# Products of a constant put into fresh PSUM tiles where a task planner foresees idle TensorE (sparse attention and non-local layer, one core)

## The chip, the cores and the metric

The kernel runs on one core of one Trainium2 chip. The metric is the device time of one execution in microseconds (us). Every run lists its own time; one execution is also recorded by the hardware profiler, and the views below (the page, the chain of waits, the timeline, the windows, the groups of instructions) are of that execution. All times in the views count from its first instruction.

## The reference

Two layers, one after the other, on an input `x` of 2 x 256 x 64 x 64 (batch, channels, height, width), all in float32. N is 64*64 = 4096.

```
# layer 0
y   = conv3x3(x, 64 output channels) ; batch norm ; PReLU          -> e  [64, N]
sim = e^T e                                                        -> [N, N]
p   = sparsemax(sim, each row)       # max(sim - tau, 0), tau from the sorted row
x   = x p + x
# layer 1
g     = x^T g_w + g_b                # [N, 128]
a, bs = (w_t theta(x)), (w_p phi(x)) # one number for each position
f     = relu(a[:, None] + bs[None, :] + wf_b)
x     = batchnorm(wz (f / N) g) + x
```

The kernel never builds most of `sim`. It takes each row of `sparsemax` as the row's own position alone unless the row has another entry near its maximum; it looks for such rows first (the survey), and works out fully only the rows that it has listed (at most 512 in a batch item). For layer 1 it sorts the `bs` of batch item 0 (and of half of item 1) by counting, so that `relu` becomes a difference of running sums; the other half of item 1 is computed as it stands. A last count says whether a dense version of everything is needed; in the runs here it is not.

## The kernel before, in words

**The planner.** The order of work is set while the kernel is built. `plan.task` (L106) records a task: a function, a cost in us on one or more engines (P is TensorE), a rank, the tasks it follows, and, for a task that opens a PSUM or a work tile, a hold on a ring (`Ring`, L79). `plan.run` (L164) is a list scheduler: at every step `begin` (L141) works out when each open task could start, and `pick` (L152) chooses; then the task's function issues its instructions.

```
    def begin(self, t, e):
        at = max(t.ready[e], self.free[e])
        if t.take:
            ...
            at = max(at, f + self.LAG)
        return at
```

So the planned start `at` is the latest of three: the engine is free, what the task follows has ended, and the ring has a free slot. Nothing of the plan's times gets into the program; only the order does. Each engine's instructions stand in that order in its own queue, and semaphores hold an instruction until its operands are there and its tile is free.

**PSUM.** `ps_sim` (L203, tag `sim`) has 3 buffers of two banks, `ps_av` (L204, tag `av`) has 2 buffers of one bank. `ring_sim` and `ring_av` (L282) stand for them in the plan. A tile's first product waits until the last reader of the buffer's earlier tile has ended.

**The stages.** Times in brackets are those of the profiled execution.

- Setup and the convolution of item 0 (`conv`, L340; products on L362 into `cv` tiles; 0 to about 66). ScalarE and VectorE take a finished pair of `cv` tiles to `e` (`scaled` L372 and L373, `outer` L378, `into_e` L383 to L388). In between, `weight_products` (L260) makes six products with one column each into the tile `pw` (L265 to L268), and `weight_biases` (L275) two into `pc`.
- The survey of item 0 (`survey`, L475; from about 44 to 199), between the tasks of item 1's convolution. Each unit is a 128 x 1024 block of `sim`: two products into a `sim` tile (`unit`, L467; products on L472, called `sv`), a running maximum by column on VectorE (L501 for the first, then L503, into `xbs`), and a sum of excess over a threshold on ScalarE (L507, in place). L512 takes rows' maxima on VectorE. `turned` (L518) transposes the maxima into `ct` (L521). `listing` (L569 to L575) makes the flags.
- The list of rows (`listed`, L580): counts in `pp` (L589 to L591), places on VectorE (L596 to L622), then eight rounds of `low_places` on VectorE (L638, `ohl`) and `numbers` on TensorE (L650, tile `pj`, two `ohl` buffers), then the indices (L656 to L660). GpSimd fetches rows of `e` and `x` (L666, L670) and masks `x` in place (`doubled`, L720).
- The listed rows (`rows`, L728): products `rw` (L472), copied to `z` by ScalarE (L745), maxima and threshold on VectorE (L748 to L762), relu (L768, L770). `attend` (L787) multiplies them into `x` (tile `av`, L794, added by L801); `project` (L817) makes `g` (L825, taken out by L831). Item 1's survey runs among these from about 208 to 349, its list around 354, its rows and `attend` from 374 to 495.
- The ranks (`Ranked`, from L932): `as_row` (L869) turns a column into a row (`pt`, L876, L880), DMA spreads it over all partitions (`kb`), and ScalarE (L992) and VectorE (L997, L1004) count for each key the keys above it (454 to 563). GpSimd scatters and fetches rows (L1026, L1112), `pk` (L1095) places, `yr` (L1132) transposes. Meanwhile TensorE does `project_in` (L845, products on L851) and the plain half, `py` (L1407), fed by ScalarE's `f` (L1397).
- The last products, `pz` (`finish`, L900; L912), are scaled and added by VectorE (L916) and stored, to 725.

The constant `onesq`, a 128 x 128 tile of ones, is written on VectorE by `constants` (L1258), before item 0's convolution is done.

Of the kernel before, what the change touches and what calls it, by code (L numbers as in the profile page):

```python
# [40 lines left out]
TH = 16  # L41
NR = 16
HH = HW // 2
PARTS = [(0, 17), (17, 33), (33, 49), (49, 64)]


# [47 lines left out]
class Plan:  # L94
# [6 lines left out]
    def __init__(self):  # L101
        self.free = {e: 0.0 for e in "PDAGS"}
        self.open = {e: [] for e in "PDAGS"}
        self.count, self.now, self.left = 0, 0.0, 0

    def task(self, cost, fn, rank=0, after=(), lat=0.0, take=None, free=None, **engines):  # L106

# [56 lines left out]
    def run(self, until=lambda: False):  # L164
        while self.left and not until():
            c = [(b[0], e, b[1]) for e in self.open for b in [self.pick(e)] if b]
            assert c, [t.fn for e in self.open for t in self.open[e]]
            at, e, t = min(c, key=lambda x: x[:2])
            for o in t.cost:
                self.open[o].remove(t)  # L170
            self.now = max(self.now, at)
            t.start, t.end, t.engine = at, at + t.cost[e], e
            self.free[e] = t.end
            self.left -= 1
            if t.take:
# [15 lines left out]
def sparse_path(ctx: ExitStack, tc, a, out, rows_i):  # L191
# [51 lines left out]
    wb = tp[:, 2].rearrange("p (d o) -> p d o", d=2)  # L243
    wc = tp[:, 3].rearrange("p (k o) -> p k o", k=CT)

    def weights():

        nc.vector.tensor_scalar_add(s1, v1[:, 4, :], EPS)
        nc.scalar.activation(s1, s1, AF.Sqrt)
        nc.vector.reciprocal(s1, s1)  # L250
        nc.vector.tensor_mul(s1, s1, v1[:, 1, :])
        nc.vector.tensor_sub(b1, v1[:, 0, :], v1[:, 3, :])
        nc.vector.tensor_mul(b1, b1, s1)
        nc.vector.tensor_add(b1, b1, v1[:, 2, :])
        for d in range(2):
            nc.vector.tensor_copy(wb[:, d], vci[:, 2 + d : 3 + d].to_broadcast([P, CI]))
        for kc in range(CT):
            nc.vector.tensor_copy(wc[:, kc], b1[:, kc : kc + 1].to_broadcast([P, CI]))

    def weight_products():  # L260


        pw = ps_av.tile([P, 2, CT + 1], F32, name="pw", tag="av")
        for kc in range(CT):
            nc.tensor.matmul(pw[:, 0, kc : kc + 1], lhsT=ph_sb[:, ts(kc, P)], rhs=vci[:, 3:4], start=True, stop=True)  # L265
            nc.tensor.matmul(pw[:, 1, kc : kc + 1], lhsT=th_sb[:, ts(kc, P)], rhs=vci[:, 2:3], start=True, stop=True)
        nc.tensor.matmul(pw[:, 0, CT : CT + 1], lhsT=wb[:, 0], rhs=vci[:, 0:1], start=True, stop=False)
        nc.tensor.matmul(pw[:, 0, CT : CT + 1], lhsT=wb[:, 1], rhs=vci[:, 1:2], start=False, stop=True)  # L268
        nc.vector.tensor_copy(gw_sb[:, :, CI], pw[:, 0, 0:CT])
        nc.vector.tensor_copy(gw_sb[:, :, CI + 1], pw[:, 0, 0:CT])  # L270
        nc.vector.tensor_copy(gw_sb[:, :, CI + 2], pw[:, 1, 0:CT])
        nc.vector.tensor_add(gb_sb[:, CI : CI + 1], pw[:, 0, CT : CT + 1], vci[:, 4:5])
        nc.vector.memset(gb_sb[:, CI + 1 : CG], 0.0)

    def weight_biases():  # L275
        pc = ps_av.tile([P, CG], F32, name="pc", tag="av")
        for kc in range(CT):
            nc.tensor.matmul(pc, lhsT=wc[:, kc], rhs=gw_sb[:, kc], start=(kc == 0), stop=(kc == CT - 1))
        nc.vector.tensor_sub(gb_sb, gb_sb, pc)
# [60 lines left out]
    def conv(b, parts, rank, ready):  # L340
# [12 lines left out]

        def taps_of(jp, g, n, j, dy):
            if (g, n, dy) == (g, 0, 1):
                d[jp, g] = ps_av.tile([P, 2, R * HH], F32, name=f"cv_{b}_{jp}_{g}", tag="av")
# [62 lines left out]
    def thresholds(b, e_of, there, rank):  # L419
# [6 lines left out]

        def turned(jp):
            e = e_of()
            ps = d[jp, "ps"] = ps_sim.tile([P, 2, 4, P], F32, name=f"tr_{b}_{jp}", tag="sim")
# [37 lines left out]
    def unit(b, e, name, lhs, q):  # L467


        ps = ps_sim.tile([P, UN], F32, name=f"{name}_{b}_{q}", tag="sim")  # L470
        for h in range(2):
            nc.tensor.matmul(ps[:, ts(h, CB)], lhsT=lhs(h), rhs=e[ts(h, CR), q], start=True, stop=True)  # L472
        return ps

    def survey(b, e_of, both, there, copied, limited, accs, rank, ready):  # L475
# [40 lines left out]
            (row_top if e == "D" else rows_over)(i, q)  # L516

        def turned(q, g, acc):  # L518
            ps = d["turn", q, g] = ps_av.tile([P, 4, P], F32, name=f"ct_{b}_{q}_{g}", tag="av")
# [60 lines left out]
    def listed(b, et, flag_of, saved, flagged, got, rank, free_mask, free_ec):  # L580
# [4 lines left out]

        def counts():
            flag = flag_of()
            pp = d["pp"] = ps_av.tile([P, 3, P], F32, name=f"pp_{b}", tag="av")
            nc.tensor.matmul(pp[:, 0, 0:NT], lhsT=tri, rhs=flag, start=True, stop=True)  # L589
            nc.tensor.matmul(pp[:, 1, 0:NT], lhsT=onesq, rhs=flag, start=True, stop=True)  # L590
            nc.tensor.transpose(pp[0:NT, 2], flag, ident)  # L591
# [52 lines left out]

        def numbers(g):
            if g == 0:
                d["pj"] = ps_av.tile([P, 3, KB], F32, name=f"pj_{b}", tag="av")
            for t in range(NT // 8):
                m = NT // 8 * g + t
                nc.tensor.matmul(  # L650
# [28 lines left out]
            nc.scalar.copy(d["eb"][:, :, 1], d["eb"][:, :, 0])  # L679

        def turned():
            pe = d["pe"] = ps_av.tile([P, KB, P], F32, name=f"pe_{b}", tag="av")
# [104 lines left out]
    def attend(b, got, done, halves, xb_ready, rank):  # L787
# [2 lines left out]

        def product(j, ct, k):
            if k == 0:
                pss[j, ct] = ps_av.tile([P, CB], F32, name=f"av_{b}_{j}_{ct}", tag="av")
# [23 lines left out]
    def project(b, ga_of, last, rank):  # L817
# [1 line left out]
        projected, d = {}, {}  # L819

        def product(m0, m1):
            ps = d[m0] = ps_av.tile([P, 3, CG], F32, name=f"g_{b}_{m0}", tag="av")
            for m in range(m0, m1):
                for kc in range(CT):
                    nc.tensor.matmul(  # L825
# [18 lines left out]

    def project_in(b, ga, m0, m1):  # L845

        ps = ps_sim.tile([P, 2, CB], F32, name=f"g_{b}_{m0}", tag="sim")
# [21 lines left out]
    def as_row(name, column, t0, nt, rank, after):  # L869
# [2 lines left out]
        d = {}  # L872

        def turned():
            d["pt"] = ps_av.tile([P, P], F32, name=f"pt_{name}_{t0}", tag="av")
            nc.tensor.transpose(d["pt"][0:nt], column()[:, t0 : t0 + nt], ident)  # L876

        def copied():
# [21 lines left out]
    def finish(b, cols, scaled, engine, rank, after, free):  # L900
# [7 lines left out]

        def product(ct):
            if ct == 0:  # L910
                d["z"] = ps_sim.tile([P, CT, CB], F32, name=f"pz_{b}_{cols.start}", tag="sim")
# [20 lines left out]
    class Ranked:  # L932
# [126 lines left out]
                nc.vector.tensor_add(at(t), at(t), at(t - 1))  # L1059

        def before(self):
            self.po = ps_av.tile([P, CB], F32, name=f"po_{self.b}", tag="av")
# [26 lines left out]
        def places(self, i):  # L1089

            b, R = self.b, self.R
            if i % 2 == 0:
                self.pk[i // 2] = ps_av.tile([P, 8, R + 1], F32, name=f"pk_{b}_{i}", tag="av")
# [25 lines left out]
        def taken(self, i, rank, rest=None):  # L1119
# [8 lines left out]

            def turned(t):
                if t % 4 == 0:  # L1130
                    d["ps"] = ps_av.tile([P, 4, P], F32, name=f"yr_{b}_{i}", tag="av")
# [124 lines left out]

    def constants():
        nc.vector.memset(onesq, 1.0)  # L1258
        nc.gpsimd.affine_select(
            out=tri, in_=onesq, pattern=[[1, P]], compare_op=ALU.is_gt, fill=0.0, base=0, channel_multiplier=-1  # L1260
        )
# [140 lines left out]

    def pair_py(q, m):
        if m == NR:
            pys[q] = ps_sim.tile([P, UN], F32, name=f"py_{q}", tag="sim")
        for h in range(2):
            nc.tensor.matmul(  # L1407
                pys[q][:, ts(h, CB)],
# [31 lines left out]
    )  # L1440
    plan.run()

    pf = ps_av.tile([1, B * (1 + KB)], F32, name="pf", tag="av")
# [395 lines left out]
```

## Time and profile before

| | before |
|---|---|
| time, median of 3 runs | 735.35 us (734.71 to 736.77) |
| the profiled execution's own time | 737.18 us |
| its span, first to last instruction | 735.4 us |
| TensorE matmul busy | 636.2 us (87%), 2783 instructions |
| VectorE / ScalarE / GpSimd busy | 559.1 us / 398.2 us / 203.5 us |
| TensorE clock granted, mean | 0.938 of full |

A float32 product appears in the profile as two MATMUL instructions and two weight loads; a transpose appears as one. "Idle before, by" in a view names what ended an engine's idle time. PEclk is the clock that TensorE was granted; in this profile it is either 1.00 or 0.50.

### The profile page before, as it was taken

Reading aid. Unit: us, or ns where it says so; the run is one execution under the profiler, and the core shown is the slowest. Engines: PE = TensorE matmul, PEld = TensorE weight load, DVE = VectorE, ACT = ScalarE, POOL = GpSimd, SP = SyncE. Lnnn points to the kernel's source line nnn. Section 1 sums busy time; section 2 is a strip of 40 time slices with the busy share of each in tenths; the row PEclk is TensorE's granted clock in tenths of the full one; section 3 lists DMA queues with packets and bytes.
Section 4 is the critical chain, followed back from the end, with each engine's and each line's share of the span. In section 5 each row is a group of like instructions: output and inputs, shape, how many; then the busy total and the mean of one; then the engine's idle time right before and its main releaser. Section 6 shows DMA issues by size and latency. Waiting matters only on the chain.

```text
span 735.4 us, 8191 instructions
## 1 busy us (share of the span) xinstructions
PE 636.2 (87%) x2783; PEld 312.3 (42%) x2783; DVE 559.1 (76%) x1025; ACT 398.2 (54%) x552; POOL 203.5 (28%) x252
## 2 busy tenths in 40 slices
PE   5989979999876979999897959996798998979683
PEld 4656444444322323333544524445443644534341
DVE  6875787677788998786746485999999987772463
ACT  0122647766555877666031352999999865414010
POOL 0006930000048000000083000152445323777240
PEclk9999999999979899999998969998899899979898
DMA  9512010001021000000110002011425345654364
GB/s 353 185 43 59 2 29 15 15 15 30 15 65 29 1 1 1 0 1 0 59 37 0 0 1 115 8 37 37 138 99 136 98 159 201 218 162 107 129 226 152
DMA packets 32984, 54.75 MB, mean 74 GB/s; under 512 B 12850, under 2 KB 19876, under 8 KB 32036
## 3 DMA queue, kind: packets, MB, share of 16 engines
q1 hardware_dynamic: 27252, 40.60, 16.5%
q0 software_dynamic: 5248, 12.94, 6.5%
q10 hardware_dynamic: 432, 0.59, 0.3%
q8 instruction: 24, 0.39, 0.2%
q14 instruction: 28, 0.23, 0.1%
HBM read 31.94 MB, written 20.07 MB: 71 GB/s over the span
## 4 chain that ended last, share of the span: by engine, by line
PE 50%; DVE 23%; ACT 12%; issue 6%; POOL 4%; DMA 4%; DVEq 0%; ACTq 0%; POOLq 0%; SPq 0%
PE sv L472 16%; ACT junk L992 9%; PE av L794 7%; PE cv_in L362 6%; PE cv_out L362 6%; PE py L1407 4%; DVE junk L997 4%; POOL r L1112 4%; DVE mq L748 4%; DVE xbs L503 4%; PE pz L912 3%; PE g L825 2%; DVE z L754 2%; DMA r<-tb,k 2%; DVE z L770 2%
## 5 line engine op out<-in xcount | busy, mean ns | idle before, releaser
L507 ACT ACTIVATE sv<-sv,nthr 128x1024 f32<-128x1024 f32 x134 | 145.9, 1090 | 93.7 <-DVE xbs L503 47.8
L472 PE MATMUL sv<-e 64*128 64x512 f32 x640 | 162.7, 627 | 7.3 <-ACT sv L507 7.3
L794 PE MATMUL av<-z,xbs 128*128 128x512 f32 x256 | 124.2, 627 | 15.5 <-DVE z L770 15.0
L503 DVE TENSOR_TENSOR xbs<-sv,xbs 128x1024 f32<-128x1024 f32 x90 | 110.1, 1224 | 29.6 <-PE sv L472 24.2
L1407 PE MATMUL py<-f,ga 128*128 128x512 f32 x256 | 120.7, 624 | 3.4 <-ACT f L1397 3.4
L992 ACT ACTIVATE junk<-kb,bound 128x640 bf16<-128x640 f32 (+30 forms) x58 | 96.5, 1665 | 8.7 <-DMA kb<-rd_k 8.7
L1397 ACT ACTIVATE f<-ab,ga 128x1024 f32<-128x1024 f32 x64 | 71.3, 1142 | 47.3 <-PE py L1407 47.2
L472 PEld LDWEIGHTS sv<-e 64*128 64x128 f32 x640 | 55.7, 189 | 92.6 <-ACT sv L507 49.9
L1026 POOL DMA_INDIRECT sg<-ga,rank x48 | 49.9, 1041 | 148.3 <-DVE junk L1004 104.0
L794 PEld LDWEIGHTS av<-z,xbs 128*128 128x128 f32 x256 | 47.5, 197 | 82.4 <-issue 55.6
L1112 POOL DMA_INDIRECT r<-tb,k x64 | 61.2, 957 | 59.1 <-PE yr L1132 20.7
L997 DVE TENSOR_SCALAR_CACHE_REDUCE junk<-kb,ga 128x128 bf16<-128x128 f32 (+29 forms) x36 | 76.6, 2162 | 0.2
L666 POOL DMA_INDIRECT eb<-et,idx x8 | 7.9, 983 | 243.8 <-DVE idx L660 129.2
L1407 PEld LDWEIGHTS py<-f,ga 128*128 128x128 f32 x256 | 49.5, 200 | 59.8 <-issue 52.7
L362 PE MATMUL cv_out<-v,wu 128*64 128x256 f32 (+1 forms) x384 | 48.8, 397 | 7.4 <-DVE v L324 7.4
L362 PE MATMUL cv_in<-v,wu 128*64 128x256 f32 (+1 forms) x384 | 49.0, 398 | 4.9 <-DVE col L524 3.9
L1125 DVE SCALAR_TENSOR_TENSOR r<-r,a 128x128 f32<-128x128 f32 x64 | 21.6, 350 | 31.3 <-DMA r<-tb,k 31.0
L801 DVE SCALAR_TENSOR_TENSOR x<-av,b,x 128x512 f32<-128x512 f32 x32 | 23.7, 747 | 27.7 <-PE av L794 26.1
L745 ACT COPY z<-rw 128x1024 f32<-128x1024 f32 x32 | 30.5, 1026 | 26.1 <-PE av L794 17.3
L362 PEld LDWEIGHTS cv_out<-v,wu 128*64 128x64 f32 x384 | 30.4, 142 | 29.0 <-issue 12.5
L912 PE MATMUL pz<-yT,wz_sb 128*128 128x512 f32 x64 | 33.3, 662 | 9.4 <-DVE yT L1139 8.1
L512 DVE MAX8 top<-sv 128x8 f32<-128x1024 f32 x26 | 32.0, 1231 | 12.2 <-PE sv L472 11.8
(202 smaller groups left out, 752.4 us busy)
## 6 DMA issues: line engine op xcount, KB each, us to landing
out<-x SPq DMA_DIRECT2D x32, 256.0 KB, 2.1
tb<-tab SPq DMA_DIRECT2D x3, 2056.0 KB
x<-in_x SPq DMA_DIRECT2D x8, 512.0 KB, 8.7
tab<-sg SPq DMA_DIRECT2D x3, 1040.0 KB, 7.6
x<-in_x SPq DMA_DIRECT2D x4, 544.0 KB
e<-e SPq DMA_DIRECT2D x16, 128.0 KB, 3.2
et<-es SPq DMA_DIRECT2D x16, 128.0 KB, 1.9
mask<-kd SPq DMA_DIRECT2D x2, 1024.0 KB, 4.6
```

The costliest lines, as they stand in the source:

```text
L362: nc.tensor.matmul(d[jp, g][ts(h, CR), n, (r0 - r) * HH : (r1 - r) * HH], lhsT=taps(j, kc, dy), rhs=v[:, kc, r0 + dy - 1 : r1 + dy - 1], s ...
L472: nc.tensor.matmul(ps[:, ts(h, CB)], lhsT=lhs(h), rhs=e[ts(h, CR), q], start=True, stop=True)
L503: nc.vector.tensor_tensor(out=acc, in0=d[i, q], in1=acc, op=ALU.max)
L507: nc.scalar.activation(ps, ps, AF.Relu, bias=both["nthr"][:, i : i + 1], accum_out=got_s["over"][:, i, q : q + 1])
L794: nc.tensor.matmul(pss[j, ct], lhsT=got["xb"][:, k, ts(ct, P)], rhs=got["zs"][k][:, ts(j, CB)], start=(k == 0), stop=(k == KB - 1),)
L912: nc.tensor.matmul(d["z"][:, ct], lhsT=wz_sb[:, ts(ct, P)], rhs=d["y"], start=True, stop=True)
L992: nc.scalar.activation(self.junk[:, 0, c0:c1], kb[:, c0:c1], AF.Sign, scale=STEEP, bias=self.bound[:, d, t : t + 1], accum_out=cnt[:, t, d ...
L997: nc.vector.tensor_scalar(self.junk[:, 1, c0:c1], kb[:, c0:c1], self.key[:, t : t + 1], None, (ALU.is_ge, ALU.is_gt)[d], ALU.add, accum_ou ...
L1026: rows = nc.gpsimd.indirect_dma_start(out=self.sg, out_offset=bass.IndirectOffsetOnAxis(ap=self.rank[:, t : t + 1], axis=0), in_=self.ga[: ...
L1112: nc.gpsimd.indirect_dma_start(out=self.r[:, t % TH], out_offset=None, in_=self.tb, in_offset=bass.IndirectOffsetOnAxis(ap=self.k[:, t : t ...
L1397: nc.scalar.activation(f[0][:, m % 4, :], ab1[0][:, ts(q, UN)], AF.Relu, bias=ga1[0][:, m, CI : CI + 1])
L1407: nc.tensor.matmul(pys[q][:, ts(h, CB)], lhsT=ga1[0][:, m, 0:CI], rhs=f[0][:, m % 4, ts(h, CB)], start=(m == NR), stop=(m == NT - 1),)
```

## The change

`Plan.run` keeps in `plan.gap` how long the chosen task's engine is planned to stand idle ahead of it. A new function `fresh` makes every PSUM tile that `ps_av.tile` or `ps_sim.tile` made before. Once `onesq` has been written (`warm` is then not empty), and where `plan.gap` is long enough, it first issues n products of `onesq` with the first columns (at most 128) of `onesq` into the new tile, each with `start=True, stop=True`. The first true product of the tile, which has `start=True` too, comes behind them and overwrites.

```
+EACH, FROM, MOST = 0.27, 0.3, 24
...
+            self.gap = at - self.free[e]
...
+    def fresh(pool, shape, dtype, name, tag):
+
+        ps = pool.tile(shape, dtype, name=name, tag=tag)
+        n = min(MOST, int((plan.gap - FROM) / EACH))
+        if n > 0 and shape[0] == P and warm:
+            v = ps
+            if len(shape) > 2:
+                axes = " ".join("abc"[: len(shape) - 1])
+                v = ps.rearrange(f"p {axes} -> p ({axes})")
+            wide = min(P, v.shape[1])
+            for _ in range(n):
+                nc.tensor.matmul(v[:, 0:wide], lhsT=onesq, rhs=onesq[:, 0:wide], start=True, stop=True)
+        return ps
+
+    warm = []
...
-        pw = ps_av.tile([P, 2, CT + 1], F32, name="pw", tag="av")
+        pw = fresh(ps_av, [P, 2, CT + 1], F32, name="pw", tag="av")
...
     def constants():
         nc.vector.memset(onesq, 1.0)
+        warm.append(True)
```

All other calls of `ps_av.tile` and `ps_sim.tile` in the sparse path are edited like that of `pw`. The planned costs and times are not touched, so the instructions of VectorE, ScalarE, GpSimd and SyncE are the same in the same order, and so are those of TensorE but for 113 added products ahead of 30 tiles. Those are, in TensorE's order (the time is that of the tile's first true product in the profile of before):

```
tile (item)       products  columns   at us      tile (item)      products  columns   at us
pw                      11        6   48.13      av_7_1 (0)              3      128  411.52
ct_3_0 (0)               6      128  182.03      rw, k=1, q=3 (1)        4      128  426.38
pp (0)                  11      128  198.99      g_30 (0)                3      128  439.69
pj (0)                   8       12  204.13      av_1_0 (1)              2      128  446.08
sv, i=1, q=1 (1)         8      128  210.64      pt (a row of item 0)    1      128  495.16
sv, next unit (1)        2      128  212.50      g_0 (1)                 1      128  495.30
rw, q=1 (0)              1      128  226.84      g_6 (1)                 5      128  497.99
rw, q=2 (0)              3      128  228.93      pt (a row of item 1)    4      128  508.02
sv, q=0 (1)              2      128  252.80      g_18 (1)                8      128  512.20
sv, q=2 (1)              5      128  265.70      py_0                    4      128  519.90
ct_3_1 (1)               3      128  350.23      py_1                    4      128  553.66
pp (1)                   1      128  354.08      pz_0 (1)                3      128  681.94
av_3_1 (0)               2      128  358.39      pz_2560 (1)             1      128  701.56
g_12 (0)                 1      128  365.67      pz_3584 (1)             1      128  707.36
g_21 (0)                 3      128  401.97      pz_3584 (0)             2      128  721.96
```

More of the change, by code (lines that the diff above doesn't have):

```diff
@@ L103, in __init__ @@
         self.open = {e: [] for e in "PDAGS"}
-        self.count, self.now, self.left = 0, 0.0, 0
+        self.count, self.now, self.left, self.gap = 0, 0.0, 0, 0.0
     def task(self, cost, fn, rank=0, after=(), lat=0.0, take=None, free=None, **engines):
@@ L275, in weight_biases @@
     def weight_biases():
-        pc = ps_av.tile([P, CG], F32, name="pc", tag="av")
+        pc = fresh(ps_av, [P, CG], F32, name="pc", tag="av")
         for kc in range(CT):
@@ L355, in taps_of @@
             if (g, n, dy) == (g, 0, 1):
-                d[jp, g] = ps_av.tile([P, 2, R * HH], F32, name=f"cv_{b}_{jp}_{g}", tag="av")
+                d[jp, g] = fresh(ps_av, [P, 2, R * HH], F32, name=f"cv_{b}_{jp}_{g}", tag="av")
             v = pair_of(b, j)
@@ L428, in turned @@
             e = e_of()
-            ps = d[jp, "ps"] = ps_sim.tile([P, 2, 4, P], F32, name=f"tr_{b}_{jp}", tag="sim")
+            ps = d[jp, "ps"] = fresh(ps_sim, [P, 2, 4, P], F32, name=f"tr_{b}_{jp}", tag="sim")
             for i in range(4):
@@ L467, in unit @@
     def unit(b, e, name, lhs, q):
-        ps = ps_sim.tile([P, UN], F32, name=f"{name}_{b}_{q}", tag="sim")
+        ps = fresh(ps_sim, [P, UN], F32, name=f"{name}_{b}_{q}", tag="sim")
         for h in range(2):
@@ L518, in turned @@
         def turned(q, g, acc):
-            ps = d["turn", q, g] = ps_av.tile([P, 4, P], F32, name=f"ct_{b}_{q}_{g}", tag="av")
+            ps = d["turn", q, g] = fresh(ps_av, [P, 4, P], F32, name=f"ct_{b}_{q}_{g}", tag="av")
             for k in range(4):
@@ L587, in counts @@
             flag = flag_of()
-            pp = d["pp"] = ps_av.tile([P, 3, P], F32, name=f"pp_{b}", tag="av")
+            pp = d["pp"] = fresh(ps_av, [P, 3, P], F32, name=f"pp_{b}", tag="av")
             nc.tensor.matmul(pp[:, 0, 0:NT], lhsT=tri, rhs=flag, start=True, stop=True)
@@ L646, in numbers @@
             if g == 0:
-                d["pj"] = ps_av.tile([P, 3, KB], F32, name=f"pj_{b}", tag="av")
+                d["pj"] = fresh(ps_av, [P, 3, KB], F32, name=f"pj_{b}", tag="av")
             for t in range(NT // 8):
@@ L681, in turned @@
         def turned():
-            pe = d["pe"] = ps_av.tile([P, KB, P], F32, name=f"pe_{b}", tag="av")
+            pe = d["pe"] = fresh(ps_av, [P, KB, P], F32, name=f"pe_{b}", tag="av")
             for k in range(KB):
@@ L792, in product @@
             if k == 0:
-                pss[j, ct] = ps_av.tile([P, CB], F32, name=f"av_{b}_{j}_{ct}", tag="av")
+                pss[j, ct] = fresh(ps_av, [P, CB], F32, name=f"av_{b}_{j}_{ct}", tag="av")
             nc.tensor.matmul(
@@ L821, in product @@
         def product(m0, m1):
-            ps = d[m0] = ps_av.tile([P, 3, CG], F32, name=f"g_{b}_{m0}", tag="av")
+            ps = d[m0] = fresh(ps_av, [P, 3, CG], F32, name=f"g_{b}_{m0}", tag="av")
             for m in range(m0, m1):
@@ L845, in project_in @@
     def project_in(b, ga, m0, m1):
-        ps = ps_sim.tile([P, 2, CB], F32, name=f"g_{b}_{m0}", tag="sim")
+        ps = fresh(ps_sim, [P, 2, CB], F32, name=f"g_{b}_{m0}", tag="sim")
         pv = ps[:, :, 0 : 3 * CG].rearrange("p d (m c) -> p d m c", c=CG)
@@ L874, in turned @@
         def turned():
-            d["pt"] = ps_av.tile([P, P], F32, name=f"pt_{name}_{t0}", tag="av")
+            d["pt"] = fresh(ps_av, [P, P], F32, name=f"pt_{name}_{t0}", tag="av")
             nc.tensor.transpose(d["pt"][0:nt], column()[:, t0 : t0 + nt], ident)
@@ L910, in product @@
             if ct == 0:
-                d["z"] = ps_sim.tile([P, CT, CB], F32, name=f"pz_{b}_{cols.start}", tag="sim")
+                d["z"] = fresh(ps_sim, [P, CT, CB], F32, name=f"pz_{b}_{cols.start}", tag="sim")
             nc.tensor.matmul(d["z"][:, ct], lhsT=wz_sb[:, ts(ct, P)], rhs=d["y"], start=True, stop=True)
@@ L1061, in before @@
         def before(self):
-            self.po = ps_av.tile([P, CB], F32, name=f"po_{self.b}", tag="av")
+            self.po = fresh(ps_av, [P, CB], F32, name=f"po_{self.b}", tag="av")
             nc.tensor.matmul(self.po[:, 0:CS], lhsT=tri, rhs=self.tab[-1][:, TH - 1], start=True, stop=True)
@@ L1092, in places @@
             if i % 2 == 0:
-                self.pk[i // 2] = ps_av.tile([P, 8, R + 1], F32, name=f"pk_{b}_{i}", tag="av")
+                self.pk[i // 2] = fresh(ps_av, [P, 8, R + 1], F32, name=f"pk_{b}_{i}", tag="av")
             for t in range(4):
@@ L1130, in turned @@
                 if t % 4 == 0:
-                    d["ps"] = ps_av.tile([P, 4, P], F32, name=f"yr_{b}_{i}", tag="av")
+                    d["ps"] = fresh(ps_av, [P, 4, P], F32, name=f"yr_{b}_{i}", tag="av")
                 nc.tensor.transpose(d["ps"][:, t % 4], self.r[:, t % TH, 0:CI], ident)
@@ L1404, in pair_py @@
         if m == NR:
-            pys[q] = ps_sim.tile([P, UN], F32, name=f"py_{q}", tag="sim")
+            pys[q] = fresh(ps_sim, [P, UN], F32, name=f"py_{q}", tag="sim")
         for h in range(2):
@@ L1441, in sparse_path @@
     plan.run()
-    pf = ps_av.tile([1, B * (1 + KB)], F32, name="pf", tag="av")
+    pf = fresh(ps_av, [1, B * (1 + KB)], F32, name="pf", tag="av")
     nc.tensor.matmul(
```

## The prediction

> **What bounds the kernel now.** I read the page first, for the share of each engine, the clock that TensorE was granted, and the chain of waits that ended last.
>
> ```profile
> PE 636.2 (87%) x2783; PEld 312.3 (42%) x2783; DVE 559.1 (76%) x1025; ACT 398.2 (54%) x552; POOL 203.5 (28%) x252
> ...
> PEclk9999999999979899999998969998899899979898
> ...
> PE 50%; DVE 23%; ACT 12%; issue 6%; POOL 4%; DMA 4%; DVEq 0%; ACTq 0%; POOLq 0%; SPq 0%
> ```
>
> TensorE is busy 87% of the span but on only half of the chain. The bound changes by stage: the chain in order of time is mostly TensorE up to about 217 us, VectorE and TensorE in turns to 446, ScalarE's and VectorE's counting (L992, L997) to 563, and then DMA, GpSimd and TensorE. So an added product costs time only where TensorE is on the chain and cannot make it up before the next thing that is late for another reason. I therefore went to the timeline at each of the 30 tiles and asked what ended TensorE's idle time there: the operand, or the release of the tile.
>
> ```profile
> 47.60 0.47 ACT L373 ACTIVATE c<-cv_in,s 128x256 f32<-128x256 f32 x1
> ...
> 48.13 0.38 PE L265 MATMUL pw<-vci,tp 128*128 128x1 f32 x2 [2.55 <-ACT c L373]
> ...
> 198.99 0.41 PE L589 MATMUL pp<-flag,tri 128*128 128x32 f32 x2 [3.24 <-DVE flag L575]
> ...
> 199.66 4.54 PE L472 MATMUL sv<-e 64*128 64x512 f32 x12
> ...
> 202.66 1.29 DVE L638 TENSOR_TENSOR ohl<-iota,lo 128x512 bf16<-128x512 f32 x2
> ...
> 204.13 0.36 PE L650 MATMUL pj<-val,ohl 128*128 128x12 bf16 x8
> ...
> 210.64 4.46 PE L472 MATMUL sv<-e 64*128 64x512 f32 x12 [2.17 <-ACT sv L507]
> ```
>
> This is the main reading. At `pp` the idle 3.24 us end with an operand (`flag`); the tile has long been free, so added products fit into the idle time. At `pw` the idle 2.55 us end when ScalarE's L373 has read the buffer's earlier `cv` tile (47.60 + 0.47 = 48.07). An added product writes that same tile, waits for that same release, and starts when the true product did: none of it fits. `sv` at 210.64 is the same (ScalarE reads the old tile, L507). The planner's gap counts both kinds, since `begin` takes the ring's release into the planned start.
>
> **What each added product costs.** No row shows `onesq` by `onesq`. The nearest is the plain float32 product of 131 columns in runs, L851: 64 products (128 instructions) in 16.9 us, 0.264 us each. The ends are the transposes of 128 columns on L521 (48 in 7.1 us, 0.148) and L825 (64 in 19.0 us, 0.297). I take 0.264. For 6 or 12 columns the nearest is `pw`'s own: six products from 48.13 to 49.63, 0.23 each; ends 0.06 (L650, 64 bf16 products in 3.8 us) and 0.46 (0.23 at half clock). The 113 products come to 94 x 0.264 + 19 x 0.23 = 29.2 us of TensorE. They issue no DMA and bring no other engine an instruction; each new wait is one that the true product behind it had.
>
> ```profile
> L851 PE MATMUL g<-gw_sb,x 128*128 128x131 f32 x128 | 16.9, 294 | 0.0
> ```
>
> **What of it lies on the path, tile by tile.**
>
> `pw`: 11 x 0.23 = 2.5 us, cover none. Behind them in TensorE's queue stand `pc` and the convolution of item 0, and the chain runs through TensorE from there. +2.5.
>
> `ct_3_0`: 6 x 0.264 = 1.6 in 1.4 us of idle before an operand. +0.2.
>
> `pp` of item 0: 11 x 0.264 = 2.9 in 3.24. +0. It also changes the clock:
>
> ```profile
> 196.86:200.28 3.42, 1.29 (x9) 0.93 (x11) 2.69 (x15) 0.19 (x2) 0.00 (x0) 1.00 0.00 0
> 200.28:203.69 3.41, 3.41 (x12) 1.22 (x8) 3.17 (x15) 0.00 (x0) 0.00 (x0) 0.50 0.38 101
> ```
>
> The columns are the stretch, its length, busy time of TensorE, weight loads, VectorE, ScalarE, GpSimd, then the granted clock. After 3.42 us with TensorE busy for 1.29, it got half the clock for 3.41 us. With the 11 products in that first stretch it should keep the full clock, and the six `sv` products at 199.66 end some 1.7 us sooner. That gain is not kept: `pj` behind them waits for `ohl`, whose first two blocks end at 202.66 + 1.29 = 203.95. But it covers the 8 x 0.23 = 1.8 us of added products at `pj`. So `pj` costs +0 if the clock holds and +1.8 if not (the flags come no sooner, and every later `ohl` goes in step with `pj`); I take 0.
>
> The two `sv` tiles at 210.64 and 212.50: 8 + 2 products, 2.6 us less 0.2, cover none on TensorE itself; VectorE's L503 waits for these units. But later something else is late:
>
> ```profile
> 224.79 12.54 POOL L720 TENSOR_TENSOR x<-x,mask 128x1024 f32<-128x1024 f32 x6
> ...
> 230.41 6.95 DVE L754 TENSOR_SCALAR z<-m 128x8 f32<-128x8 f32 x1
> ```
>
> An operation of VectorE on 8 elements takes 6.95 us and ends at 237.36, when GpSimd's burst ends at 237.33; elsewhere this line takes 0.23. It happens again (386.33 to 393.03, GpSimd to 393.00). GpSimd's burst follows the indices (L660) without a pause, not the survey. So a delay of VectorE's chain up to some 6.7 us that comes after the indices is swallowed there. The 2.4 us: +0, and the same for the two `rw` tiles of item 0. If it is not swallowed, +2.4.
>
> `sv`, q=0, at 252.80 (2): VectorE's maxima (L748) are back to back there, +0. `sv`, q=2, at 265.70 (5): its wait is for ScalarE's reading of the old tile; VectorE then goes back to back through L503 to 284, so a late start is not made up. 5 x 0.264 - 0.17 = +1.15.
>
> `ct_3_1` (3), item 1's `pp` (1) and `av_3_1` (2): TensorE is full, and `pj` and item 1's indices follow, so GpSimd's second burst moves too. 0.8 less 0.35 of idle behind `ct`, then 0.26 and 0.53: +1.2. `g_12` (1) comes when the indices are nearly done; the second burst swallows it.
>
> `g_21`, `av_7_1` and `g_30`, 3 each: TensorE is full from 402 to 417 and on the chain, and from 440 the keys of the ranks wait for `g_30`. 9 x 0.264 = +2.4. `rw` at 426.38 (4): VectorE's L748 is back to back, +0. `av_1_0` (2): behind the transpose that the ranks wait for, but ahead of the `av` products that fill TensorE from 446; +0.4.
>
> The other 11 tiles, from 495 on, hold 34 products, 9.0 us. To 563 ScalarE's and VectorE's counting is late, not TensorE; then fetched rows and `yT`, which end the idle time of 0.75 to 1.23 us ahead of the last three `pz` tiles. +0. If that cover is gone, what does not fit into idle time is 0.2 + 0.3 + 1.3 + 2.1 + 1.1 + 0.8 = 5.8 us.
>
> Sum: 2.5 + 0.2 + 1.15 + 1.2 + 2.4 + 0.4 = 7.85 us. The profiled execution took 737.18 us (span 735.4), so 745.0 against itself; the median before is 1.83 below that execution, so I forecast 735.35 + 7.85 = 743.2 us.
>
> **The clock, weighed.** Half-clock stretches in which the chain runs on TensorE, by the windows and the chain: 50.1, 101.3, 200.3 and 210.6 (3.4 us each), 396.1 (5.6), 439.9 (2.7), 569.1 (6.7), 661.4 (3.1) and 690.6 (4.6), 36 us together. At full clock they would take half, so 18 us is all that the clock can return. Of the 30 tiles only `pp` fills the quiet time ahead of such a stretch; the products at `pw` start after theirs, and have 6 columns. The convolution's idle stretch before 101.3, the relu stage before 396.1 and the waits for rows before 569, 661 and 690 get nothing.
>
> The Trainium skill, page "TensorE: Matmul & The Clock Gate", section "Part 1: The HAM clock gate", says of such ramps: "For modeling, the ramp penalty is <1% of a typical kernel span". An estimate by it puts the whole prize under 7.4 us, less than my sum of costs, so by the page alone filling idle time could not pay here even if it kept every window warm. The rows of this trace differ: they show 18 us, 2.4%.
>
> **Rivals.** First, the covers fail (chance 0.15): the delayed survey is not swallowed (+2.4), the clock at 200.3 falls all the same (+1.8), and the small products at `pw` run at half clock (+2.5, from 0.46 each): 7.85 + 6.7 = 14.6, 749.9 us. For it: narrow products before 50.1 did not keep the clock. Against: three things at once.
>
> Second, the products are cheap (chance 0.12): with one and the same constant as weights they cost the low ends, 0.148 and 0.06. Then `pw` 0.7, `ct_3_0` 0, `sv` 0.6, the stage around 354 0.5, the three at 402 to 440 1.3, `av_1_0` 0.1: 3.2 us, 738.6.
>
> Third, the other side (chance 0.07): the gate. If the added products keep the clock up on the listed stretches, the kernel gains up to 18 us against 7.85, ending at 725. It turns faster than before once more than 7.85 of the 18 come back, about four of the nine stretches. For it: the stretch after `pp`. Against: only that one has its quiet time filled, and its gain ends in a wait for `ohl`.
>
> That the change does not do what it says is excluded for the count (the built program has the 113 products), not for the place: ahead of 14 of the 30 tiles the trace has no idle time where the plan foresees some.
>
> **How the numbers follow.** The sum has 0.66; the rivals 0.15, 0.12 and 0.07. A measurement here can tell about 0.3%, 2.2 us. The sum and the first rival are slower by more; the second gives 738.6 but reaches down into no change with half its chance; the third is faster. So faster 0.07, the same 0.06, slower 0.87. The range goes from just below the cheap products to just short of the failed covers, 738.0 to 749.0.
>
> **What would show it.** In the profile after: a new group for the line in `fresh`, 226 MATMUL instructions; at `pw`, 2.5 us of them from about 48.1 after an unchanged wait; around `pp`, no idle time and a full clock where 200.3 was half; the long VectorE instruction on L754 shorter by about what the survey lost; from 446 on a shift that stays constant. It is wrong if the mean clock rises from 0.938 to above 0.96 with the half-clock stretches at 396, 569 or 690 gone, if the new group takes under 0.2 us a product, or if the shift grows after 495.

## The result and the profile after

| | before | after |
|---|---|---|
| time, median (runs taken side by side) | 735.03 us (734.29 to 736.77, 4 runs) | 743.59 us (742.59 to 744.80, 4 runs) |
| ratio, 95% interval | 1 | 1.0114 (1.0089 to 1.0139) |
| the profiled execution's own time, span | 737.18, 735.4 us | 744.80, 743.0 us |
| TensorE clock granted, mean | 0.938 | 0.943 |

The change costs 8.6 us by the medians; the sum said 7.85. The total is right to a microsecond, but several terms of it are not, and gains that the sum did not have stand against them. Ratios here and below compare executions in the chip's fast state; a slower one showed in one later session alone. First the page of the changed kernel: engines, clock, chain.

```profile
PE 660.6 (89%) x3009; PEld 342.9 (46%) x3009; DVE 553.5 (74%) x1025; ACT 398.5 (54%) x552; POOL 204.2 (27%) x252
...
PEclk9988989999989989999989988998999899989998
...
PE 55%; DVE 28%; issue 5%; ACT 4%; POOL 4%; DMA 3%; DVEq 0%; ACTq 0%
```

TensorE has 226 instructions more and the other engines have as many as before. The share of TensorE on the chain rises from 50% to 55%, and the clock hardly moves.

**At `pw`.** The timeline of the changed kernel, TensorE only (start, length, line, operation, in brackets the idle time before it), and then the windows of the gate, which is what grants TensorE its clock: the stretches of 3.41 us at whose ends the clock changes (busy time of TensorE, weight loads, VectorE, ScalarE and GpSimd, then the clock):

```profile
48.48 3.06 PE L259 MATMUL pw<-onesq 128*128 128x6 f32 x22 [2.56 <-ACT c L391]
51.40 0.56 PE L283 MATMUL pw<-vci,tp 128*128 128x1 f32 x2
...
54.53 1.21 PE L296 MATMUL pc<-gw_sb,tp 128*128 128x131 f32 x4 [0.43 <-PE pw L286]
```

```profile
47.08:50.49 3.41, 2.00 (x18) 2.01 (x19) 1.50 (x3) 2.94 (x7) 0.00 (x0) 1.00 0.00 0
50.49:53.91 3.42, 3.42 (x18) 3.42 (x17) 0.00 (x0) 0.00 (x0) 0.00 (x0) 0.50 0.00 0
53.91:57.32 3.41, 2.98 (x13) 1.80 (x13) 3.08 (x12) 0.00 (x0) 0.00 (x0) 0.50 0.02 5
57.32:60.73 3.41, 3.41 (x23) 2.02 (x23) 2.70 (x9) 0.59 (x1) 0.00 (x0) 0.50 0.92 207
```

The 11 products wait as long as `pw`'s true product did before (2.56 against 2.55 us), then take 3.06 us. The new and dear part is the clock: before, half clock held from 50.1 for 3.4 us; now it holds from 50.5 to 60.7, three windows. In the first of these TensorE is busy without a pause, and still gets half the clock in the next. For comparison, before's window from 50.09 to 53.50 was as busy (3.41 of 3.41 us, at half clock too) and the next had the full clock. Set start against start, the same instructions come 4.5 us later behind `pw`, 5.8 us later from 58 us on, and 6.9 us later from 105 on, where half clock holds for two windows (105.1 to 111.9) and before had one (101.3 to 104.7). 0.3 us of it is there ahead of `pw`.

**At `pp` and `pj`.** The timeline of the changed kernel:

```profile
202.55 2.72 PE L259 MATMUL pp<-onesq 128*128 128x128 f32 x22
...
205.87 0.41 PE L607 MATMUL pp<-flag,tri 128*128 128x32 f32 x2 [0.59 <-DVE flag L593]
...
209.31 1.95 PE L259 MATMUL pj<-onesq 128*128 128x12 f32 x16
209.54 1.29 DVE L656 TENSOR_TENSOR ohl<-iota,lo 128x512 bf16<-128x512 f32 x2
...
211.12 0.34 PE L668 MATMUL pj<-val,ohl 128*128 128x12 bf16 x8
```

Idle time before the first true `pp` product falls from 3.24 to 0.59 us. The clock is full through this stretch, `pj`'s eight products fit ahead of `ohl`, and the indices come 7.0 us later than before; the flags ahead of `pp` had come 6.9 us later.

**The swallowed delay.** Further on in the changed kernel, one view of TensorE, one of GpSimd, one of VectorE:

```profile
217.61 3.73 PE L259 MATMUL sv<-onesq 128*128 128x128 f32 x16 [2.18 <-ACT sv L525]
```

```profile
231.77 12.56 POOL L738 TENSOR_TENSOR x<-x,mask 128x1024 f32<-128x1024 f32 x6
```

```profile
239.88 4.48 DVE L772 TENSOR_SCALAR z<-m 128x8 f32<-128x8 f32 x1
244.40 0.17 DVE L774 TENSOR_TENSOR_SCAN cs<-onesq,z 128x8 f32<-128x8 f32 x1
```

The eight products in `sv` took 0.47 us each, since they stand at half clock. VectorE's chain is 9.5 us late at L772 (239.88 against 230.41), GpSimd's burst 7.0. The small operation takes 4.48 us instead of 6.95, which is the difference, and ends with the burst again (244.36 and 244.33). What follows it is 7.0 late: the loss at `sv` is gone.

**From there to the end.** At `sv`, q=2, the shift goes from 7.0 to 9.7, by 366 us to 10.5, falls to 7.8 at 402, is 9.1 behind `g_21` and `av_7_1`, 8.8 at 455 and 7.6 at the end.

### The profile page after: what moved, and what is told of

Same layout as the page of the kernel before. It is cut to its first block, busy times and chain, and to the rows that moved or that the text cites. A ratio compares the mean times of both kernels' runs of the same rounds, so it can differ in the third digit from the quotient of the medians.

```text
span 743.0 us, 8644 instructions
## 1 busy us (share of the span) xinstructions
PE 660.6 (89%) x3009; PEld 342.9 (46%) x3009; DVE 553.5 (74%) x1025; ACT 398.5 (54%) x552; POOL 204.2 (27%) x252
## 4 chain that ended last, share of the span: by engine, by line
PE 55%; DVE 28%; issue 5%; ACT 4%; POOL 4%; DMA 3%; DVEq 0%; ACTq 0%
PE sv L490 16%; PE av L812 13%; DVE junk L1015 7%; PE cv_in L380 7%; PE cv_out L380 6%; POOL r L1130 4%; DVE mq L766 4%; PE pz L930 3%; DVE xbs L521 3%; DMA r<-tb,k 2%; PE g L843 2%; PE py L1426 2%; DVE z L788 2%; DVE z L772 1%; DVE tab L1084 1%
## 5 line engine op out<-in xcount | busy, mean ns | idle before, releaser
L490 PE MATMUL sv<-e 64*128 64x512 f32 x640 | 158.6, 615 | 4.3 <-ACT sv L525 4.3
L380 PE MATMUL cv_in<-v,wu 128*64 128x256 f32 (+1 forms) x384 | 51.2, 412 | 4.9 <-DVE col L542 3.9
L380 PEld LDWEIGHTS cv_in<-v,wu 128*64 128x64 f32 x384 | 31.7, 148 | 25.0 <-issue 15.7
```

What stands on the lines that cost most here:

```text
L380: nc.tensor.matmul(d[jp, g][ts(h, CR), n, (r0 - r) * HH : (r1 - r) * HH], lhsT=taps(j, kc, dy), rhs=v[:, kc, r0 + dy - 1 : r1 + dy - 1], s ...
```

## The experiments

In all of these but the one on the planner's gap, the formula in `fresh` is replaced by a table of products for each tile; the rest is the changed kernel. Only what differs from that is shown, and names of tiles are shortened.

```
-        n = min(MOST, int((plan.gap - FROM) / EACH))
+        n = MINE.get(name, 0)
```

Theory: an added product costs where the tile's release ends the idle time, and only if what is late next is not late for another reason. The rivals are those of the prediction.

### The products at pw

Three kernels: the change without them, they alone, and they alone but 128 columns wide.

```
 e1  MINE = the 30 tiles' numbers, without pw
 e2  MINE = {"pw": 11}
 e7  MINE = {"pw": 11}
-    pw = fresh(ps_av, [P, 2, CT + 1], F32, name="pw", tag="av")
+    pw = fresh(ps_av, [P, 2, CB // 2], F32, name="pw", tag="av")
```

Expected without them: 

> The change without the 11 products at pw; the other 102 stay, by name and number. The sum prices pw at 2.5 us, so by it this is 741.1, 2.5 below the change. The rival that the profile after suggests: the six-column products also leave two half-clock stretches behind (53.9 to 60.7), so pw is worth 5.5 to 6 us and this is about 738.

Expected of them alone: 

> The kernel before with the 11 products at pw and no others. By the sum 735.0 + 2.5 = 737.5; by the rival (half clock behind them) 740.5 to 741. If later stretches of half clock shift about, the difference to before need not be the mirror image of the run without pw.

Expected of the wide ones: 

> As the run with pw alone, but its tile has 256 columns, so that the 11 products are 128 wide. If the clock falls behind narrow products because they keep the array too little busy, the two extra half-clock stretches go, and it costs 11 x 0.264 = 2.9 us or less (the half-clock stretch of before at 50.1 may go too, worth 1.7 us): 736.2 to 738. If the delay costs whatever the products' width, it is no faster than the run with the narrow ones.

Measured: 1.0038 (1.0019 to 1.0057) without them, 1.0052 (1.0031 to 1.0072) with them alone, 1.0002 (0.9985 to 1.0018) with them wide. So the narrow products are worth 3.8 us alone (2.3 to 5.3) and, as the difference of the whole and the part (1.0114 less 1.0038, times 735), 5.6 us in the change (some 3.3 to 7.9, both intervals together). The run alone does not exclude the sum's 2.5; the difference does, and the traces do: between the start of `pw` and 58 us the shift grows by 5.4 us in the changed kernel and by 6.8 in the kernel with the narrow products alone. That one then gets 2.7 us back at 396 (last section of the experiments), which is why its time shows less. Its windows:

```profile
48.80:52.20 3.40, 2.95 (x14) 2.96 (x15) 0.88 (x2) 1.98 (x5) 0.00 (x0) 0.50 0.00 0
52.20:55.60 3.40, 3.40 (x17) 3.40 (x17) 0.00 (x0) 0.00 (x0) 0.00 (x0) 0.50 0.00 0
55.60:59.00 3.40, 2.97 (x13) 2.44 (x15) 2.23 (x10) 0.00 (x0) 0.00 (x0) 0.50 0.02 5
59.00:62.40 3.40, 3.40 (x22) 1.74 (x20) 2.72 (x8) 0.59 (x1) 0.00 (x0) 0.50 0.66 150
```

Then the timeline and the windows of the kernel with the wide ones:

```profile
48.70 2.72 PE L261 MATMUL pw<-onesq 128*128 128x128 f32 x22 [2.55 <-ACT c L393]
```

```profile
47.49:50.90 3.41, 2.20 (x19) 2.21 (x20) 1.30 (x3) 2.74 (x7) 0.00 (x0) 1.00 0.00 0
50.90:54.31 3.41, 2.98 (x27) 2.65 (x27) 1.55 (x9) 0.00 (x0) 0.00 (x0) 1.00 0.02 5
```

Eleven products of 128 columns take 2.72 us, 0.247 each; narrow ones take about as long (the eight of 12 columns at `pj`, at full clock, 1.95 us or 0.244 each). In the window with the first of the products TensorE is about as busy either way (2.20 and 2.00 of 3.41 us), but after the wide ones there is no half-clock stretch at 50 us at all, and the narrow ones, busy for a whole window, did not end one. The shift of the kernel with the wide ones is 3.1 us at `pw` and 1.7 us at 105, 0.6 of it there ahead of `pw`. What wide products pay is about what they earn.

The length of the stretch at 50 us depends on more than the products. In the traces of the eleven kernels without added products at `pw` it is one window ten times, and two in the kernel with the middle alone (49.2 to 56.0). With the narrow ones it is three and four, with the wide ones none. So one window more can come without them; two and three more were seen with the narrow ones only.

### The two sv tiles

```
 e3  MINE = {"sv3_1_1": 8, "sv4_1_1": 2}
```

Expected: 

> The kernel before with the 8 and 2 products at the two sv tiles near 210 and no others. My theory (GpSimd's burst, which VectorE's L754 waits out, swallows the delay): VectorE's L503 some 2.4 to 3.7 us late at 214, nothing late after 237.4, time of before within 0.3%. The rival (not swallowed): 2.4 to 3.7 us longer.

Measured: 0.9998 (0.9980 to 1.0016). VectorE's line of this kernel:

```profile
232.29 4.71 DVE L775 TENSOR_SCALAR z<-m 128x8 f32<-128x8 f32 x1
```

It starts 1.9 us later than before's 230.41, takes 2.2 less than 6.95, and from there to `sv`, q=2, nothing is late. Swallowed, as the sum had it. At `sv`, q=2, where this kernel has no added product, a half-clock stretch (261.1 to 267.9) that before does not have makes the work 1.3 us later; 1.1 us of it is made up at 396.

### The middle alone

```
 e6  MINE = {sv q=2: 5, ct_3_1: 3, pp of item 1: 1, av_3_1: 2,
             g_21: 3, av_7_1: 3, g_30: 3, av_1_0: 2}
```

Expected: 

> The kernel before with the products at sv q=2 (5), ct_3_1 (3), pp of item 1 (1), av_3_1 (2), g_21 (3), av_7_1 (3), g_30 (3) and av_1_0 (2), no others. By the sum 1.15 + 1.2 + 2.4 + 0.4 = 5.2 us longer. The rival from the profile after: the shift there is set by where half-clock stretches fall (five products at sv q=2 at half clock cost 2.7, the stretch at 396 was gone for a gain of 2.6), so anything from 2 to 6.

Measured: 1.0065 (1.0042 to 1.0089), 4.8 us. The terms of the sum for these eight tiles make 1.15 + 1.2 + 2.4 + 0.4 = 5.15. The time agrees, the trace does not bear it out: 2.4 us of shift arise between 46 and 105 us, ahead of the first added product, where half clock holds for two windows twice; `sv`, q=2, adds 1.1, the tiles around 354 0.8, `g_21` and `av_7_1` 1.3, and `g_30` and `av_1_0` nothing (-0.2), 3.0 in all. Here `sv`, q=2, stands at full clock (the timeline of this kernel) and costs 1.1 to 1.3 us; in the changed kernel it stands at half clock (the timeline of that) and costs 2.7.

```profile
267.80 1.38 PE L268 MATMUL sv<-onesq 128*128 128x128 f32 x10 [1.11 <-ACT sv L534]
```

```profile
273.18 2.34 PE L259 MATMUL sv<-onesq 128*128 128x128 f32 x10
```

### The eleven late tiles alone

```
 e5  MINE = the numbers of the 11 tiles from 495 us on, 34 in all
```

Expected: 

> Only the 11 tiles from 495 us on keep their 34 added products (9.0 us of TensorE); the other 19 tiles have none. The prediction's sum (covered by the counting to 563 us and by operands that come late after it): +0, within 1 us of before. If the cover is gone: +5.8 us. A third reading, from the traces of before and after, in which the shift fell from 8.8 to 7.6 us behind 495: the products also keep some clock, so 1.2 us faster than before; the half-clock stretches then lie elsewhere than before's 569 and 690.

Measured: 0.9990 (0.9973 to 1.0007), a change of -0.7 us (-2.0 to +0.5). The 9.0 us of TensorE are covered; +5.8 is excluded, and whether they earn a little cannot be told.

### The gap counted from the later of engine and slot

```
-            self.gap = at - self.free[e]
+            slot = 0.0
+            if t.take and len(t.take.ring.holds) >= t.take.ring.n:
+                slot = t.take.ring.holds[-t.take.ring.n].freed + self.LAG
+            self.gap = at - max(self.free[e], slot)
```

Expected: 

> The change, but the planner's gap counts idle time only from the later of engine free and ring slot free. That leaves 14 of the 30 tiles: ct_3_0, pp and pj of item 0, and 11 from 495 on without the two at the front of that list (pt of item 0, py_1, pz_0): none that waits for a release. By my sum 0.2 + 0 + 0: the time of before within 0.3%. If the cover of the tiles from 495 on is not there, up to 5 us longer; if the clock pays, some 1 to 3 us shorter.

What was built has 51 products ahead of 11 tiles, not the 14 that the expectation names. Measured: 0.9993 (0.9970 to 1.0015). With the products behind a release gone, and `pw`'s with them, no loss is left that the runs can tell, and nothing is won. The prediction's distinction, operand or release, is what the planner's gap lacked.

### Idle time filled

Here the numbers come from the trace instead of the plan: tiles that are free ahead of their operand, filled to about the length of the idle time.

```
 e4   MINE = {ct_3_0: 4, pp: 11, av_0_0: 19,
              pt of item 1: 24, pt_k: 4, py_0: 11,
              pk: 9, yr: 4, pz: 18, 4, 4, 2}
 e8   e4, and 27 products into a spare sim tile while item 1's
      threshold is worked out (around 429 to 442 us)
 e11  the first line of e4     e12  the second     e10  the third
```

Expected of all of it: 

> Products only at tiles that were free long before their operand in the profile of before, as many as the idle time there holds at 0.27 us (ct_3_0 4, pp 11, av_0_0 19, pt of item 1 24, pt_k of item 1 4, py_0 11, pk_0 9, yr_3 4, pz_1024 18, pz_2560 4, pz_3584 4 and 2). By my theory they cost nothing, and return clock only where TensorE is on the chain right behind: at 569 (up to 3.3 us) and 690 (up to 2.3); 729.5 to 735. The rival that the gate is worth little: 735, no change. The rival that the plan's idle time is real and the gate pays everywhere: below 728.

Expected with the threshold's idle time filled too: 

> The run that filled only tiles free ahead of their operand, and besides 9 and 18 products into a spare sim tile ahead of the third and fourth product of av_0_0 of item 1 (idle 2.98 and 5.26 us before, for z). If a product there keeps the gate up, the stretch at half clock behind 429 goes, worth up to 1.4 us: 0 to 1.5 us faster than that run. If the spare tile's release is late, or the idle time is shorter than in the profile of before, up to 2 us slower.

Expected of the early tiles: 

> Of the tiles of the filled kernel only the three early ones: 4 products at ct_3_0, 11 at item 0's pp, 19 at item 0's first av tile, each in idle time that an operand ends. By the theory of swallowed shifts, the time that TensorE saves at 200 and 240 us is lost again in waits for VectorE and GpSimd: the end within 1 us of before, unless the windows fall so that the half-clock stretch of before's 394.8 to 401.7 us lies elsewhere; then 2.8 us faster from 396 us on, kept to 446 us and to the end. If filling by itself is what pays, wherever it stands: 1.7 us or more faster already at 211 us.

Expected of those in between: 

> Of the filled kernel's tiles only the three between the early and the late ones: 24 products at the transposed row of item 1 (pt), 4 at the row of keys (pt_k), 11 at py_0, all between 497 and 520 us, each in idle time that an operand ends. If the gains of the filled kernel's parts add up (0.9935 in all, 0.9978 from the three early tiles, 1.0002 from the late ones), about 0.9955 is left for these, 3.3 us. If what the late parts earn depends on where the gate's windows fall, these alone give nothing, since the counting to 563 us ends later than TensorE: within 1 us of before.

Expected of the late tiles: 

> Of the tiles of the filled kernel only the late ones: 9 products at the place tile pk, 4 at the transposes of fetched rows (yr), and 18, 4, 4 and 2 ahead of four pz tiles, 41 in all, each in idle time that an operand ends. If the gain of the filled kernel comes from filling, at the place where the products stand: the quiet window at 566 us is busy, the stretch at 569 runs at full clock and the end comes 2.5 to 3.5 us earlier than before. If it came from where the gate's windows happened to fall at 396 us, nothing of it is here: within 1 us of before.

Measured: all 0.9935 (0.9911 to 0.9958), 731.97 us against 736.91, so faster than before and than the change; with the threshold's idle time 0.9941 (0.9918 to 0.9964); the early tiles 0.9978 (0.9965 to 0.9991); those in between 0.9961 (0.9924 to 0.9998), from runs that scatter between 741.9 and 749.7 us where before took 743.2 to 753.2 beside them; the late ones 1.0002 (0.9987 to 1.0016).

At `pk` the filling does what it should, with all tiles as with the late ones alone. The windows of before, then of the kernel with all tiles:

```profile
568.93:572.34 3.41, 3.27 (x16) 3.27 (x16) 3.27 (x11) 3.41 (x5) 2.96 (x5) 0.50 0.64 166
572.34:575.75 3.41, 3.41 (x6) 1.65 (x7) 3.24 (x10) 0.67 (x2) 0.14 (x2) 0.50 0.30 73
```

```profile
565.90:569.31 3.41, 3.41 (x29) 3.17 (x29) 3.27 (x11) 3.41 (x6) 2.96 (x5) 1.00 0.54 169
569.31:572.72 3.41, 3.41 (x13) 1.49 (x11) 3.27 (x10) 3.41 (x7) 0.24 (x2) 1.00 0.28 65
```

The stretch of 6.8 us is gone, and TensorE gains 3.3 us between 569 and 576 (2.9 with the late tiles alone). But with the late tiles alone it is not kept: at 624 us 0.4 us of it are left. The windows of that kernel:

```profile
619.58:623.00 3.42, 0.18 (x1) 0.00 (x0) 1.54 (x5) 0.99 (x1) 2.51 (x4) 1.00 0.40 107
623.00:626.41 3.41, 2.97 (x14) 3.00 (x15) 2.50 (x5) 0.00 (x0) 2.69 (x3) 0.50 0.42 116
626.41:629.80 3.39, 3.39 (x7) 1.84 (x8) 3.32 (x5) 0.00 (x0) 2.59 (x3) 0.50 0.39 97
```

TensorE waits for GpSimd's fetched rows there, as before it did, but now a whole window is quiet, and two windows of half clock follow where before had one (626.95 to 630.36). The theory held at its place and failed for the total.

With the threshold's idle time filled the mean clock is the highest of all (0.962, against 0.953 without), and the half-clock stretch at 429 to 442 shrinks from 13.6 to 3.4 us; the time is the same. VectorE sets the pace there, and its work takes the same at either clock of TensorE (four maxima 4.60 us from 432.82, at full clock, and 4.60 us from 440.15, at half, in the changed kernel). So filling paid nothing there, ahead of work that TensorE is not late with.

Of the 4.9 us that all tiles gain (736.91 to 731.97), the trace shows 2.7 arising at 396 to 402 and 3.3 at 569 to 576; the span of the profiled execution is 4.7 us shorter (730.7 against 735.4). The 2.7 are no idle time filled in its place: between 238 and 497 us this kernel has no added product (next section). Whether the three parts simply add up stays open: their product, 0.9941, lies on the 0.9935 of the whole, but the interval of the middle part is too wide to show it.

### What happens at 396 us

This came out of the traces of several of these kernels, and it explains the fall of the shift from 10.5 to 7.8 in the changed kernel. Ahead of the products of `g` at 396, TensorE waits for VectorE, which waits for GpSimd's second burst. The timeline of before, of the kernel with all idle time filled, and of the changed kernel:

```profile
396.06 2.99 PE L825 MATMUL g<-gw_sb,x 128*128 128x131 f32 x12 [4.34 <-DVE x L801]
```

```profile
395.91 1.61 PE L856 MATMUL g<-gw_sb,x 128*128 128x131 f32 x12 [1.50 <-DVE x L832]
```

```profile
406.59 1.61 PE L843 MATMUL g<-gw_sb,x 128*128 128x131 f32 x12 [1.48 <-DVE x L819]
```

The wait is shorter by just what the burst has swallowed. In both kernels VectorE is 2.84 us later at 371 us, against before, than behind the burst (+2.69 against -0.15; +13.38 against +10.53 or 2.85), and 4.34 - 2.84 = 1.50. This delay is not made of added products: it is a half-clock stretch that lies ahead of the burst there, from 364.5 to 371.3 with all idle time filled and from 374.8 to 381.6 in the changed kernel. The windows of before, of the filled and of the changed kernel:

```profile
349.00:381.00 32.00, 29.53 (x139) 16.00 (x139) 17.78 (x46) 4.07 (x7) 12.41 (x11) 1.00 0.17 50
```

```profile
364.50:367.90 3.40, 2.66 (x16) 2.57 (x16) 1.37 (x5) 0.00 (x0) 1.18 (x2) 0.50 0.02 5
```

```profile
374.80:378.20 3.40, 2.51 (x17) 2.36 (x18) 1.70 (x6) 0.00 (x0) 0.99 (x1) 0.50 0.00 0
378.20:381.60 3.40, 3.40 (x10) 2.23 (x10) 0.57 (x1) 0.00 (x0) 2.65 (x3) 0.50 0.14 29
```

Before has the full clock there and half clock from 394.8 to 401.7 instead. In the filled kernel 12 instructions of `g` from 365.51 take 2.99 us, as those at 396 did before. In the kernels with the early tiles alone, with the middle alone and with the wide `pw`, 1.7 us are swallowed, and the wait is 2.6 to 2.7 us, near 4.34 - 1.7. These three have one window of half clock ahead of the burst and one behind it. So the stretch has moved from behind the burst, where it counts, to ahead of it, where the burst hides it: the delay pushes TensorE's work up against the end of the burst, the quiet time ahead of the next products becomes shorter, and these run at full clock: 12 instructions in 1.61 us instead of 2.99. Of the 2.7 us of it in the changed kernel, no part is a product that was put there. One execution of each kernel is traced; how often the stretch falls on which side, and whether early filling is what moves it, is not shown.

## Why the prediction was right or wrong, point by point

- **The reading, operand or release.** Right, and the loss comes from the second kind: `pw` and the middle tiles, whose idle time a release ends or which have none, cost (of the middle ones not all: `g_30` and `av_1_0` cost nothing in the traces); `pp` and the late ones do not. A gap counted from the slot's release costs nothing that the runs can tell (0.9993).
- **The price.** Right: 0.23 to 0.29 us a product at full clock, over the tiles with four or more, against 0.264 and 0.23. The second rival, cheap products, is out. What the price lacked was the clock: 0.47 at half clock, for the 13 products at the first `sv` tile and at `sv`, q=2.
- **`pw`, +2.5.** The step that failed. The sum priced 11 products and left the clock as it was; the runs put the term at 3.8 (alone) to 5.6 us (in the change), the trace of the change at 5.4 by 58 us. The first rival had this as one of its three parts ("the small products at `pw` run at half clock", +2.5, so 5.0), and the prediction had seen that they have 6 columns and would not hold the clock. It did not see that the half clock would also be prolonged for `pc` and the convolution behind them; one of the two further windows can come without the products, as the kernel with the middle alone shows.
- **`pp` and `pj`, +0.** Right in the shift and in the clock; 0.59 us of idle time were left where none was foreseen.
- **The two `sv` tiles, +0.** Right for the reason given, and tried alone; the first rival's second part (+2.4) is out. The delay itself was 2.7 instead of 2.4.
- **`sv`, q=2, +1.15.** Right where it stands at full clock (1.1 to 1.3), mis-sized in the changed kernel (2.7), where a half-clock stretch had moved under it; in the kernel with the two `sv` tiles alone such a stretch cost 1.3 there without a product.
- **The rest of the middle, 1.2 + 2.4 + 0.4.** Too large: 0.83 + 1.34 - 0.26 = 1.9 in the trace of the changed kernel, and as much in that of the middle alone. `g_30` and `av_1_0`, priced at 0.8 + 0.4, did not reach the path. That the middle alone measured 4.8 against 5.15 is in part luck, since 2.4 us of shift stand in its trace ahead of its first product.
- **The clock at 396, not foreseen.** "Of the 30 tiles only `pp` fills the quiet time" was right on products and wrong on the conclusion: a half-clock stretch can move to where its cost is hidden, for 2.7 us. The total agreed with the sum because errors cancel, which is luck. By the traces of before and after: 0.3 ahead of `pw`, 5.4 at `pw` (the sum had 2.5), 1.1 at 105 (nothing), 0.1 from `ct_3_0` to `pj` (0.2), 2.7 at `sv`, q=2 (1.15), 1.9 in the rest of the middle (4.0), -2.7 at 396 and -1.2 behind 455 (nothing for both), 7.6 in all, the shift at the end. The medians differ by 8.6.
- **From 495 on, +0.** Right in that nothing was lost; the shift falls there from 8.9 to 7.6, where "a shift that stays constant" was forecast from 446 on.
- **The other side, the gate.** In the changed kernel the mean clock went up by 0.005 only, and the 569 and 690 stretches came back at 579.6 and, half as long, at 699.0; only the one at 396 is gone, and it came back at 374.8, where it costs nothing. Filling can pay all the same, if the idle time is the trace's: 0.9935 with 114 products, against 1.0114 with 113 where the planner put them. But only the gain at 569 to 576 arises where products fill a quiet stretch; the other is the stretch that moved.
- **The page's rule on the clock.** The estimate from the Trainium skill, page "TensorE: Matmul & The Clock Gate", section "Part 1: The HAM clock gate", put the whole prize under 7.4 us and so let filling fail. The page's sentence is on the ramp at the start of sustained matmuls in a typical kernel; to set it against stretches that come back nine times on the chain asked more of it than it says. The kernel with idle time filled won 4.9 us, which lies below both that and the 18 us counted on the rows, and does not decide between them.

## What to carry to other kernels

Idle time ahead of an instruction can take filling only if an operand ends it; where a buffer's release ends it, anything written into that buffer first stands on the path, so a planner's gap has to be counted from the later of engine and slot. Follow a delay to the next place that is late for another reason before adding it to a sum: there it disappears, and it may even close the quiet time that costs the clock. Warm a clock with wide products (128 columns here), since narrow ones took as long, and only ahead of work that this engine is late with. Before a gain is put down to filling, look whether it arises where the products stand.

## What the runs showed of the hardware

- Products of 6 columns took 0.28 us each, partly at half clock, and with `pw`'s own of one column behind them kept TensorE busy for 3.42 of 3.42 us by the profile, and the next window had half the clock; before's window of convolution products, 3.41 of 3.41 us at half clock, was followed by the full clock, and with 128 columns instead of 6 there was no half clock there at all. So in these traces the profile's busy time alone does not tell what the clock will be.
- A half-clock stretch is one or several windows of 3.41 us (3.4, 6.8, 10.2 and 13.6 us in these traces). An added delay moves the work against them, so the same five products cost 1.38 us in one kernel and 2.34 in another.
- VectorE's 8-element operation ended with GpSimd's burst in each of the four kernels where it was read off (before, after, the two `sv` tiles alone, idle time filled), whenever it started within the burst, after 3.85 to 6.97 us. The Trainium skill, page "SBUF — State Buffer", section "SBUF: two separate sides", says that VectorE and GpSimd share a pair of ports, an exclusive lock held for one whole instruction. One `x<-x,mask` instruction takes 12.56 / 6 = 2.1 us here, so if the lock were passed on after the instruction that holds it, the wait would be at most 2.1 us, an estimate by that rule; the rows show up to 6.97, across several instructions of the burst. That it is this lock, and why it would not have been passed on, was not tried.
